# A quarter of the sums by source beside the filling of layer 0's slots, and layer 3's target factors spread over partitions by transfers

## The chip, the cores and the metric

The kernel runs on one core of one Trainium2 chip. The metric is the device time of one execution in microseconds, as the median of several runs; less is better. Of one execution there is also a profile, which the hardware profiler took; its times are microseconds from the start of the span. Engines are called PE (TensorE matmul), PEld (TensorE weight load), DVE (VectorE), ACT (ScalarE), POOL (GpSimd) and SP (SyncE, which here only issues transfers).

## The reference, cut to what matters

A graph network of four layers on 3125 nodes of 256 features and 100000 edges. Each layer adds a graph part and a mixing part, and then a feed-forward part, to x. Two pieces concern the change.

Layer 0's feed-forward part sends every node to its two best of 16 experts:

```python
topk_vals, topk_idx = jax.lax.top_k(gate_logits, K)          # K = 2, E = 16
topk_w = jax.nn.softmax(topk_vals, axis=-1)
h = jax.nn.relu(jnp.einsum('bsh,ehf->bsef', x, w1) + b1)
expert_out = jnp.einsum('bsef,efh->bseh', h, w2) + b2
moe = jnp.sum(topk_w[..., None] * sel, axis=2)               # sel: the two chosen experts' outputs
```

Layer 3's graph part is attention over edges with 4 heads of 64:

```python
e = jax.nn.leaky_relu(a_src[src] + a_dst[dst], 0.2)
alpha = softmax of e over the edges of each dst
out = jax.ops.segment_sum(alpha[:, :, None] * xp[src], dst, num_segments=n)
```

Layer 2's graph part needs, per source node, the sum of |edge_weight| over its edges. These are the "sums by source"; they depend on the inputs alone, so the kernel may compute them at any time before layer 2.

## The kernel before, in words

Nodes are kept as 25 blocks of 125 on partitions. `x` and `xn` are `[125, 25, 256]` tiles that live throughout; `xt` is the transposed copy. Columns are also cut into seven pieces: six of 500 nodes and one of 125. The kernel is written in a tile framework: the program text gives every instruction's place, and when the program is built a planner orders each engine's instructions by an estimate of when they can run, in case of doubt by their place in the text. On the chip each engine then works through its own list in that order. PSUM tiles named `ps` come from one pool of four banks, through `self.bank()`.

**Filling of layer 0's slots** (`l0_ffn`). The gates are sorted into slots: one tile of 384 slots belongs to one expert, and there are 26 tiles. A chain of small DVE operations ends in `slot` (L1113). POOL then issues 50 indirect transfers (L1116), which scatter the 25 blocks of `xn`, twice each, to `b0x_d` in memory. Meanwhile `times_rows` forms gates times the second bias and adds it to `xn` in place: per piece it transposes the gates (L290), copies them to `gt` (L162 or L164), multiplies (L296) and adds (L297). L297 overwrites `xn`, so it follows the scatters of its block.

**The tile loop** follows. For tile i, SP loads the expert's weights and the tile's rows (L1139 to L1145; the order on SP is written out by hand here), PE transposes the rows (L1150), DVE copies them (`xbt`, L1152), PE multiplies by w1 (L260), ACT applies Relu (L1157), PE multiplies by w2 (L1162), DVE and ACT copy the result (`yb`, L162 and L164), and ACT's queue stores it.

**The sums by source** (`weights_by_source`) run beside the tile loop as a generator. It loads sources and weights (L513, L515), prepares keys and three bf16 parts of the weights on DVE (L520 to L532), and then works through 782 columns of edges in 196 groups of four columns: `lo`, `oh` and three `ow` on DVE (L536 to L542), four matmuls of 128x128 by 75 on PE (L544), all into one accumulating bank. Pool `w_wk` holds three `lo`, `oh` and `ow` each. After every tile the loop lets it go on to the share (i + 1) / 26. Its DVE instructions are kept behind `filled`, the last L297.

**Layer 3's dense stage** (`l3_gnn_mix`, `l3_dense`). Edge counts have been laid out as a dense matrix `ctt_d`. For two pieces of target nodes (1000 columns) at a time, two heads at a time, the loop over 25 source blocks loads counts `cs` (L155, L156, three buffers), forms `t` by Relu on ACT (L1951), `z` on DVE (L1954), and multiplies by `xr` on PE into four accumulators (L1957). `rows`, which lies in the memory of `xn`, holds the target factors exp(0.8 a_dst + bias) of all four heads for the present pair, the same on all 125 partitions. They are made ahead of every pair: PE multiplies `xt` by the attention column, broadcast over the weights' columns (L1930), and ACT applies Exp (L1932). At the end of two heads, accumulators are copied, transposed (L1972) and finished on DVE (L1912 to L1919). The last pair is one piece of 125, taken with all four heads. A second generator, the mixing part, runs beside it: `together` lets the two alternate by their progress, the mixer ahead by a factor of 1.15.

Of the kernel before, what the change touches and what calls it, by code (L numbers as in the profile page):

```python
# [12 lines left out]
F32 = mybir.dt.float32  # L13
# [4 lines left out]
AF = mybir.ActivationFunctionType  # L18
OP = mybir.AluOpType
# [4 lines left out]
N = 3125  # L24
D = 256
P = 125
NB = 25
HB = D // 128
# [9 lines left out]
PW = 500  # L38
# [52 lines left out]
def _tables():  # L91


    t = np.zeros((NT1 * 128, 4), np.float32)
    t[:, 0] = N
    n = 0
    for b, (r, ws) in enumerate(WINDOWS):
        for d, w, k in ws:
            for j in range(k):
                t[n] = b * P + d, w, r, 128 * j  # L100
                n += 1
    t = np.concatenate([t, np.zeros((128, 4), np.float32)])
    t[NT1 * 128:, 0] = N
    t[NT1 * 128:NT1 * 128 + NB, 0] = np.arange(NB) * P
    return np.ascontiguousarray(t.reshape(NT1 + 1, 128, 4).transpose(1, 2, 0))
PIECES = [(i, min(PW, N - i)) for i in range(0, N, PW)]


class Net:
    NE, TS = 16, 384  # L110
# [938 lines left out]
    def l0_ffn(self, fast=False):  # L1049

        nc, tc, a = self.nc, self.tc, self.a
        NE, TS, ST, NT, bx = self.NE, self.TS, self.TS // 128, self.NT, self.bx
        by = self.dram.tile([NT * TS, D], F32, name="b0y_d")
        with ExitStack() as s:
            sb = s.enter_context(self.pool("f0_sb"))
            wk = s.enter_context(self.pool("f0_wk", 2))
            b2 = sb.tile([NE, D], F32, name="b2")
# [3 lines left out]
            g, w, i8 = self.top2(sb, None, NE, P, NB, self.greatest)  # L1061
# [17 lines left out]
            for e in range(NE):  # L1079
                nc.vector.tensor_tensor_scan(run[:, :, e], self.ones[:, :NB], tot[:, :, e], 0.0,  # L1080
                                             op0=OP.mult, op1=OP.add)
# [4 lines left out]
                                    op0=OP.mult)  # L1086
# [21 lines left out]
            slot = sb.tile([P, 2, NB], I32, name="slot")  # L1108
            sf = sb.tile([P, 2, NB], F32, name="slotf")
            for j in range(2):  # L1110
                nc.vector.tensor_mul(hot[j], hot[j], run[:P])
                nc.vector.tensor_reduce(sf[:, j, :], hot[j], axis=AX.X, op=OP.add)
            nc.vector.tensor_scalar(slot, sf, float(NT * TS - 1), None, op0=OP.min)  # L1113
            for b in range(NB):
                for j in range(2):
                    st = nc.gpsimd.indirect_dma_start(  # L1116
# [3 lines left out]
                    tc.add_to_no_dep_group("slots", st.ins)  # L1120
            self.add_rows(beta)
            y = self.xn
            filled = self.times_rows(sb, g, b2, NE, y, self.xn)
            with ExitStack() as s2:
                sums = None
                if fast:
                    sums = self.weights_by_source(s2.enter_context(self.pool("w_sb")),
                                                  s2.enter_context(self.pool("w_wk", 3)), self.bank())
                wk2 = s2.enter_context(self.pool("f0_t", 3))
                pl = s2.enter_context(self.pool("f0_ps", 4, space=PSUM))  # L1130
                s2.enter_context(tc.manual_schedule(engines={mybir.EngineType.SP}))

                def bank():
                    return pl.tile([128, 512], F32, name="pl")

                for i in range(NT):
                    e = nc.sync.value_load(own[0:1, i:i + 1], min_val=0, max_val=NE - 1)
                    w1 = wk2.tile([128, HB, 512], F32, name="w1")
                    nc.sync.dma_start(w1, a["L0_ffn_w1"][ds(e, 1)].rearrange("o (c p) f -> p (o c) f", p=128))  # L1139
                    b1 = wk2.tile([128, 4], F32, name="b1")  # L1140
                    nc.sync.dma_start(b1, a["L0_ffn_b1"][:, ds(e, 1), :].rearrange("p o f -> p (o f)"))
                    w2 = wk2.tile([128, 4, D], F32, name="w2")
                    nc.sync.dma_start(w2, a["L0_ffn_w2"][ds(e, 1)].rearrange("o (c p) f -> p (o c) f", p=128))
                    xb = wk2.tile([128, ST, D], F32, name="xb")
                    nc.sync.dma_start(xb, bx[i * TS:(i + 1) * TS].rearrange("(t p) d -> p t d", p=128))  # L1145
                    xt = wk2.tile([128, HB, TS], F32, name="xbt", bufs=2)
                    for h in range(HB):
                        ps = bank()
                        for t in range(ST):
                            nc.tensor.transpose(ps[:, t * 128:(t + 1) * 128], xb[:, t, h * 128:(h + 1) * 128],  # L1150
                                                self.ident)
                        nc.vector.tensor_copy(xt[:, h, :], ps[:, :TS])  # L1152
                    hid = wk2.tile([128, 4, TS], F32, name="hid", bufs=2)
                    for f in range(4):
                        ps = bank()
                        self.mm_feat(ps[:, :TS], w1[:, :, f * 128:(f + 1) * 128], xt, 0, TS)
                        nc.scalar.activation(hid[:, f, :], ps[:, :TS], AF.Relu, bias=b1[:, f:f + 1])  # L1157
                    yb = wk2.tile([128, ST, D], F32, name="yb", bufs=2)
                    for t in range(ST):
                        ps = bank()  # L1160
                        for f in range(4):
                            nc.tensor.matmul(ps[:, :D], hid[:, f, t * 128:(t + 1) * 128], w2[:, f, :],  # L1162
                                             start=(f == 0), stop=(f == 3))
                        self.evac(yb[:, t, :], ps[:, :D])
                    nc.scalar.dma_start(by[i * TS:(i + 1) * TS].rearrange("(t p) d -> p t d", p=128), yb)
                    if sums is not None:

                        with tc.issue_after(filled.ins):
                            for part in sums:
                                if i + 1 < NT and part > (i + 1) / NT:  # L1170
                                    break

            def gather(i, w_):
                for b in range(i // P, (i + w_) // P):
# [659 lines left out]
    def l3_gnn_mix(self, before, arrivals):  # L1834
# [5 lines left out]
        nc, a = self.nc, self.a  # L1840
        with ExitStack() as s:
            ms = s.enter_context(self.pool("m3_sb"))
            with self.pool("m3_w") as sb:
                w = self.load_w(sb, "L3_gnn_W")
# [36 lines left out]
            nc.vector.tensor_reduce(self.viol[:P, 6:7], over, axis=AX.X, op=OP.add)  # L1881
            nc.vector.tensor_tensor(bias, a8, bias, op=OP.min)

            us = sb.tile([P, 3, NB, 4], F32, name="us")
            nc.vector.tensor_sub(us[:, 2], al[:, :, :4], top[:, :, :4].to_broadcast([P, NB, 4]))
            nc.scalar.activation(us[:, 0], us[:, 2], AF.Exp)
            nc.scalar.activation(us[:, 1], us[:, 2], AF.Exp, scale=0.2)
            nc.vector.tensor_scalar(us[:, 2], us[:, 1], -1.0, None, op0=OP.mult)
            mix.send(mw)
            self.together([self.l3_dense(sb, wk, pa, wx, xr, us, bias), mix], (1.0, 1.15))  # L1890

    def together(self, parts, pace=(1.0, 1.0)):

# [5 lines left out]
            except StopIteration:  # L1899
                del at[p]  # L1900

    def l3_dense(self, sb, wk, pa, wx, xr, us, bias):

        nc = self.nc
        few = sb.tile([P, NB, 4], F32, name="few")
# [4 lines left out]
        def finish(b, h0, nh, acc):  # L1910
# [8 lines left out]
            nc.vector.scalar_tensor_tensor(v, t[:, :nh].rearrange("p h d -> p (h d)"), 0.0, v,  # L1919
                                           op0=OP.max, op1=OP.add)  # L1920

        done, there = 0, []
        for p0 in range(0, len(PIECES), 2):
            pcs = PIECES[p0:p0 + 2]
            n = sum(w for _, w in pcs)
            for h in range(4):
                for k, (i, w) in enumerate(pcs):
                    ps = self.bank()
                    for c in range(HB):
                        nc.tensor.matmul(ps[:P, :w], wx[:, c, 260 + h:261 + h].to_broadcast([128, P]),  # L1930
                                         self.xt[:, c, i:i + w], start=(c == 0), stop=(c == HB - 1))
                    nc.scalar.activation(rows[:, h, k * PW:k * PW + w], ps[:P, :w], AF.Exp, bias=bias[:, h:h + 1],  # L1932
                                         scale=0.8)
            hg = 4 if n < PW else 2
            for h0 in range(0, 4, hg):
                acc = {}
# [3 lines left out]
                for b in range(NB):  # L1940
# [20 lines left out]
                    if b == 5:  # L1961
                        for i in there:
                            self.arrive(i)
                        there = []
                if hg == 2:
                    for h in range(2):
                        for k, (i, w) in enumerate(pcs):
                            self.evac(at[:, h, k * PW:k * PW + w], acc[h, k][:, :w])
                    for j in range(n // P):
                        ps = self.bank()  # L1970
                        for h in range(2):
                            nc.tensor.transpose(ps[:P, h * 65:(h + 1) * 65], at[:, h, j * P:(j + 1) * P],  # L1972
                                                self.ident[:65, :65])
                        finish(p0 * 4 + j, h0, 2, ps[:P, :130].rearrange("p (h c) -> p h c", h=2))
                        yield done / (NB * N * 4)
                else:
                    for h in range(4):
                        self.evac(at[:, h // 2, h % 2 * P:(h % 2 + 1) * P], acc[h, 0][:, :P])
                    ps = self.bank()
                    for h in range(4):  # L1980
                        nc.tensor.transpose(ps[:P, h * 65:(h + 1) * 65], at[:, h // 2, h % 2 * P:(h % 2 + 1) * P],
                                            self.ident[:65, :65])
                    finish(p0 * 4, 0, 4, ps[:P, :260].rearrange("p (h c) -> p h c", h=4))
# [426 lines left out]
```

## Time and profile before

| | us |
|---|---|
| median of 3 runs | 4722.29 (4718.48 to 4723.53) |
| profiled execution | 4857.34 |
| its span | 4855.5 |
| PE busy in the span | 3791.1 (78%) |
| DVE busy | 2518.8 (52%) |
| ACT busy | 1321.2 (27%) |
| POOL busy | 1016.0 (21%) |
| L544, sums by source, on PE | 76.3 between 888 and 1290 |
| L1116, 50 scatters on POOL | 59.6 between 807 and 888 |
| L1930, target factors on PE | 47.3 |
| L1932, target factors on ACT | 17.3 |
| granted TensorE clock, mean | 0.859 |

A group of instructions in the profile is given by its line, engine and operation, what it writes and reads, shapes and count; then busy time and mean duration; then the idle time of the engine just before it and what ended that. Records of TensorE count a float32 product twice. A line can be that of a helper: L155, L162, L164, L260 and L297 serve many stages, so they are read by stretch of time.

### The profile page before, as it was taken

Reading aid. Unit: us, or ns where it says so; the run is one execution under the profiler, and the core shown is the slowest. Engines: PE = TensorE matmul, PEld = TensorE weight load, DVE = VectorE, ACT = ScalarE, POOL = GpSimd, SP = SyncE. Lnnn points to the kernel's source line nnn. Section 1 sums busy time; section 2 is a strip of 40 time slices with the busy share of each in tenths; the row PEclk is TensorE's granted clock in tenths of the full one; section 3 lists DMA queues with packets and bytes.
Section 4 is the critical chain, followed back from the end, with each engine's and each line's share of the span. In section 5 each row is a group of like instructions: output and inputs, shape, how many; then the busy total and the mean of one; then the engine's idle time right before and its main releaser. Section 6 shows DMA issues by size and latency. Waiting matters only on the chain. (4 is left out here: it accounts for less than half of the span.)

```text
span 4855.5 us, 50596 instructions
## 1 busy us (share of the span) xinstructions
PE 3791.1 (78%) x16806; PEld 2521.4 (52%) x16806; DVE 2518.8 (52%) x8603; ACT 1321.2 (27%) x2364; POOL 1016.0 (21%) x1041
## 2 busy tenths in 40 slices
PE   1886895799657899997454556676599999999798
PEld 0675894566534565555343445455364444444465
DVE  5886335445576319954222222343355667667544
ACT  1466100111123232333000000000154655556511
POOL 1000002200243000002666666666000000000011
PEclk8786996799878799998676777787799999999799
DMA  6245511433230000002333333333301112111132
GB/s 181 59 119 145 137 33 40 127 119 118 82 80 19 24 14 7 14 7 65 90 94 92 93 92 92 86 93 92 111 7 31 51 44 59 42 49 52 50 128 68
DMA packets 253461, 352.56 MB, mean 73 GB/s; under 512 B 61645, under 2 KB 198276, under 8 KB 253191
## 3 DMA queue, kind: packets, MB, share of 16 engines
q1 hardware_dynamic: 133326, 169.77, 12.1%
q0 software_dynamic: 62832, 126.93, 9.9%
q10 hardware_dynamic: 57033, 52.54, 4.0%
q8 instruction: 137, 2.24, 0.2%
q14 instruction: 133, 1.09, 0.1%
HBM read 262.48 MB, written 94.92 MB: 74 GB/s over the span
## 5 line engine op out<-in xcount | busy, mean ns | idle before, releaser
L1598 POOL DMA_INDIRECT hg<-hx_d,idx x782 | 743.0, 950 | 418.8 <-issue 209.7
L1614 PE MATMUL acc<-hg,to 128*125 128x256 f32 x2042 | 590.7, 445 | 280.7 <-issue 157.7
L1614 PEld LDWEIGHTS acc<-hg,to 128*125 128x125 f32 x2042 | 439.3, 222 | 411.1 <-issue 192.7
L1957 PE MATMUL acc<-z,xr 125*65 125x500 f32 (+1 forms) x1400 | 573.7, 552 | 10.5 <-DVE z L1954 8.6
L1609 DVE TENSOR_SCALAR to<-iota_w,rel_b,kw 128x125 f32<-128x125 f32 (+1 forms) x782 | 252.7, 378 | 454.9 <-remote 263.6
L1954 DVE SCALAR_TENSOR_TENSOR z<-t,us,cs 125x1000 f32<-125x1000 f32 (+1 forms) x400 | 410.2, 1029 | 136.2 <-PE acc L1957 103.3
L1951 ACT ACTIVATE t<-xn,us 125x1000 f32<-125x1000 f32 (+1 forms) x400 | 409.4, 1037 | 236.9 <-DVE z L1954 231.3
L1957 PEld LDWEIGHTS acc<-z,xr 125*65 125x65 f32 x1400 | 187.8, 143 | 313.2 <-issue 271.3
L260 PE MATMUL ps<-xt,w 128*128 128x500 f32 (+1 forms) x672 | 268.8, 547 | 1.8 <-DMA w<-in_L_ffn_W_dram 1.8
L1533 DVE SCALAR_TENSOR_TENSOR junk<-iota_w,rel_b,lock 128x125 f32<-128x125 f32 (+1 forms) x782 | 248.0, 384 | 0.0
L796 ACT ACTIVATE k<-k 125x128 f32<-125x128 f32 x50 | 15.8, 317 | 775.1 <-DVE k L795 542.8
L2240 POOL DMA_INDIRECT bx_d<-row,slot x25 | 31.2, 1247 | 923.3 <-ACT t L1951 809.4
L588 PE MATMUL ps<-y,cb 125*125 125x256 bf16 x1875 | 215.2, 280 | 0.0
L588 PEld LDWEIGHTS <-cb 125*125 125x125 bf16 x1875 | 214.0, 141 | 0.1
L189 ACT ACTIVATE rstd_t<-rstd_t 125x4 f32<-125x4 f32 (+2 forms) x86 | 17.2, 203 | 678.6 <-DVE rstd_t L188 622.1
L254 PE MATMUL ps<-wo,h 128*125 128x256 f32 x800 | 187.7, 386 | 3.6 <-ACT h L1436 2.6
L1442 DVE SCALAR_TENSOR_TENSOR x<-ps,lg,x 125x256 f32<-125x256 f32 x200 | 92.7, 480 | 173.5 <-PE ps L254 173.5
L260 PEld LDWEIGHTS ps<-xt,w 128*128 128x128 f32 x672 | 122.7, 193 | 114.5 <-issue 102.2
L260 PE MATMUL ps<-h,w 128*128 128x500 f32 (+1 forms) x448 | 179.5, 541 | 2.3 <-ACT h L1431 1.6
L254 PEld LDWEIGHTS ps<-wo,h 128*125 128x125 f32 x800 | 142.7, 187 | 66.0 <-ACT h L1436 43.7
L260 PE MATMUL pl<-xbt,w 128*128 128x384 f32 x416 | 169.9, 557 | 8.2 <-DVE xbt L1152 5.8
L469 PE MATMUL t<-ky,lo 128*128 128x75 bf16 (+4 forms) x1251 | 138.5, 253 | 38.6 <-ACT ct L472 24.5
(566 smaller groups left out, 6225.3 us busy)
## 6 DMA issues: line engine op xcount, KB each, us to landing
cs<-ctt_d SPq DMA_DIRECT2D x150, 218.8 KB
w<-in_L_ffn_w_dram SPq DMA_DIRECT2D x52, 512.0 KB
cnt_d<-cd SPq DMA_DIRECT2D x25, 683.6 KB
cb<-cnt_d SPq DMA_DIRECT2D x25, 683.6 KB
ctt_d<-ct ACTq DMA_DIRECT2D x6, 2734.4 KB
hg<-hx_d,idx POOLq DMA_INDIRECT x782
b0x_d<-zero SPq DMA_DIRECT2D x1, 9984.0 KB
xb<-b0x_d SPq DMA_DIRECT2D x26, 384.0 KB
```

The source lines that it names most:

```text
L254: self.nc.tensor.matmul(ps, xt[:, h, b * P:(b + 1) * P], w[:, h, :], start=(h == 0), stop=(h == k - 1))
L260: self.nc.tensor.matmul(ps, w[:, h, :], xt[:, h, i:i + n], start=(h == 0), stop=(h == k - 1))
L469: nc.tensor.matmul(t[:, w * 25 * r:(w + 1) * 25 * r], lo[:, :, n % 4], ky[:, :25 * r, n % 4], start=(j == 0), stop=(j == ws[w0 + w][2] - 1))
L588: nc.tensor.matmul(ps[:P, :D], cf[k][:, h * P:(h + 1) * P], y3[:, b0 + k, j, :], start=(k == 0 and j == 0), stop=(k == m - 1 and j == 2))
L1442: nc.vector.scalar_tensor_tensor(self.x[:, b, :], ps[:P, :D], g[:, b, e:e + 1], self.x[:, b, :], op0=OP.mult, op1=OP.add)
L1533: nc.vector.scalar_tensor_tensor(junk[:, :m * P], self.iota_w[:, :m * P], rel[:, c:c + 1], lock[:, b:b + m].rearrange("p b n -> p (b n)"), ...
L1598: nc.gpsimd.indirect_dma_start(out=hg[:, j, :], out_offset=None, in_=hx, in_offset=bass.IndirectOffsetOnAxis(ap=idx[:, c0 + j:c0 + j + 1], ...
L1609: nc.vector.tensor_scalar(to, self.iota_w[:, :nb * P], rel[:, c:c + 1], kw[:, j:j + 1], op0=OP.is_equal, op1=OP.mult)
L1614: nc.tensor.matmul(acc[k], to[:, (k - b) * P:(k - b + 1) * P], hg[:, j, :D], start=(c == first[k]), stop=(c == last[k]))
L1951: nc.scalar.activation(t[:, :n], rows[:, k4, :n], AF.Relu, bias=us[:, 2, b, k4:k4 + 1], scale=us[:, 0, b, k4:k4 + 1])
L1954: nc.vector.scalar_tensor_tensor(z[:, :n], t[:, :n], us[:, 1, b, k4:k4 + 1], c, op0=OP.add, op1=OP.mult)
L1957: nc.tensor.matmul(acc[h, k][:, :w], xr[:, b, k4, :], z[:, k * PW:k * PW + w], start=(b == 0), stop=(b == NB - 1))
```

## The change

Two parts.

The first part begins the sums before the tile loop. Their DVE instructions are now kept behind `placed`, the operation that writes `slot`, and not behind the last L297. Ahead of the tile loop, and outside the part in which SP's order is written out by hand, the generator is driven until its share exceeds `EARLY` = 0.25. In the loop, the shares run from there to 1.

The second part makes the target factors once: four exponentials of `[125, 25]` from `al`, a transpose, a copy and a store of `[100, 125]` to a tensor `r3_d` in memory. `target_rows` then loads 1000 columns of two heads from there, broadcast over 125 partitions, by SP: all four heads ahead of the first pair, and from then on two heads for the next pair, as soon as these heads of the present pair are through. The products L1930 and exponentials L1932 go.

```diff
+EARLY = 0.25
...
-            nc.vector.tensor_scalar(slot, sf, float(NT * TS - 1), None, op0=OP.min)
+            placed = nc.vector.tensor_scalar(slot, sf, float(NT * TS - 1), None, op0=OP.min)
...
-            filled = self.times_rows(sb, g, b2, NE, y, self.xn)
+            self.times_rows(sb, g, b2, NE, y, self.xn)
             with ExitStack() as s2:
                 sums = None
                 if fast:
                     sums = self.weights_by_source(s2.enter_context(self.pool("w_sb")),
                                                   s2.enter_context(self.pool("w_wk", 3)), self.bank())
+
+                    with tc.issue_after(placed.ins):
+                        for part in sums:
+                            if part > EARLY:
+                                break
...
-                    if sums is not None:
-
-                        with tc.issue_after(filled.ins):
-                            for part in sums:
-                                if i + 1 < NT and part > (i + 1) / NT:
-                                    break
+                    for part in sums or ():
+                        if i + 1 < NT and part > EARLY + (1 - EARLY) * (i + 1) / NT:
+                            break
...
+            r = sb.tile([P, 4, NB], F32, name="r3")
+            for h in range(4):
+                nc.scalar.activation(r[:, h], al[:, :, 4 + h], AF.Exp, bias=bias[:, h:h + 1], scale=0.8)
+            ps = self.bank()
+            nc.tensor.transpose(ps[:4 * NB, :P], r.rearrange("p h b -> p (h b)"), self.ident[:P, :P])
+            rt = sb.tile([4 * NB, P], F32, name="rt3")
+            nc.vector.tensor_copy(rt, ps[:4 * NB, :P])
+            r_d = self.dram.tile([4, N], F32, name="r3_d")
+            nc.sync.dma_start(r_d.rearrange("h (b p) -> (h b) p", p=P), rt)
+
             us = sb.tile([P, 3, NB, 4], F32, name="us")
...
-            self.together([self.l3_dense(sb, wk, pa, wx, xr, us, bias), mix], (1.0, 1.15))
+            self.together([self.l3_dense(sb, wk, pa, xr, us, r_d), mix], (1.0, 1.15))
...
+        def target_rows(i, h0):
+
+            n = min(2 * PW, N - i)
+            for h in (h0, h0 + 1):
+                if n > 0:
+                    self.move(nc.sync, rows[:P, h, :n], r_d[h, i:i + n].partition_broadcast(P))
+
         done, there = 0, []
+        for h0 in (0, 2):
+            target_rows(0, h0)
         for p0 in range(0, len(PIECES), 2):
             pcs = PIECES[p0:p0 + 2]
             n = sum(w for _, w in pcs)
-            for h in range(4):
-                for k, (i, w) in enumerate(pcs):
-                    ps = self.bank()
-                    for c in range(HB):
-                        nc.tensor.matmul(ps[:P, :w], wx[:, c, 260 + h:261 + h].to_broadcast([128, P]),
-                                         self.xt[:, c, i:i + w], start=(c == 0), stop=(c == HB - 1))
-                    nc.scalar.activation(rows[:, h, k * PW:k * PW + w], ps[:P, :w], AF.Exp, bias=bias[:, h:h + 1],
-                                         scale=0.8)
...
                 if hg == 2:
+                    target_rows(pcs[0][0] + 2 * PW, h0)
                     for h in range(2):
```

`move` issues two transfers for one tile: partitions 0 to 111, and the rest.

More of the change, by code (lines that the diff above doesn't have):

```diff
@@ L1900, in together, with l3_dense @@
                 del at[p]
-    def l3_dense(self, sb, wk, pa, wx, xr, us, bias):
+    def l3_dense(self, sb, wk, pa, xr, us, r_d):
         nc = self.nc
```

## The prediction

> **What bounds the kernel now.** I read the busy time by stretch first, then the groups of instructions, then the order of events on single engines. The change touches three stretches: the filling of the slots (807 to 888 us), the tile loop (888 to 1290) and layer 3's dense stage (3676 to 4590). Columns: busy us and (instructions) of PE, PEld, DVE, ACT, POOL, granted TensorE clock, DMA share, GB/s.
>
> ```profile
> 807.00:888.00 81.00, 28.95 (x63) 13.08 (x63) 14.58 (x31) 1.69 (x3) 59.64 (x50) 0.50 0.36 101
> 888.00:1290.00 402.00, 376.19 (x1924) 276.96 (x1925) 204.65 (x1058) 73.92 (x141) 0.00 (x0) 0.93 0.37 117
> 3676.00:3696.00 20.00, 18.58 (x44) 8.21 (x45) 5.29 (x12) 11.69 (x18) 0.00 (x0) 0.91 0.05 13
> 3696.00:4510.00 814.00, 800.71 (x2422) 354.18 (x2421) 547.31 (x1052) 471.01 (x534) 20.45 (x16) 1.00 0.19 49
> ```
>
> In the fill POOL issues 50 scatters back to back and everyone else idles. The tile loop has PE busy 376 of 402 us, the dense stage 801 of 814: both end when PE ends, and PE time taken out of them is time gained. The next lines are PE groups: busy us, mean ns, then idle before the group.
>
> ```profile
> L544 PE MATMUL ps<-ow,lo 128*128 128x75 bf16 x752 | 76.3, 249 | 17.4 <-DVE ow L542 15.6
> L1957 PE MATMUL acc<-z,xr 125*65 125x500 f32 (+1 forms) x1400 | 573.7, 552 | 10.5 <-DVE z L1954 8.6
> L1930 PE MATMUL ps<-xt,wx 128*125 128x500 f32 (+1 forms) x112 | 47.3, 587 | 0.9 <-DVE rd L1914 0.9
> ```
>
> L544 is the sums by source, L1930 the product that spreads the target factors. Who waits in the fill:
>
> ```profile
> DVE xn L297 <- DMA b0x_d<-xn,slot: 65.5, 25, 6.4
> PE ps L296 <- DVE xn L297: 18.4, 13, 2.2
> ```
>
> DVE's add L297 overwrites xn, so it waits for the scatters that read it, one block each 2.95 us; L296 waits in turn for the add to free one of the four shared banks.
>
> **What the Trainium skill says.** "SBUF — State Buffer", Who interferes with whom: a tensor_tensor has no mode that takes the port pair shared with GpSimd, copies, casts and tensor_scalars may. The sums' groups are tensor_tensor; only preparation (three casts, two tensor_scalars and a key cast, each 0.56 us) could hold up a scatter, 3.4 us at worst. No such overlap is in this trace. "TensorE: Matmul & The Clock Gate", Part 1: an idle PE runs at half clock; the fill's 0.50 agrees. "DMA: Bandwidth & Descriptors", Anatomy of one DMA: about 2.0 us plus bytes over 436 GB/s. The first xb load (384 KB) took from its issue at 884.61 to PE's start at 888.15, 3.5 us against an estimate of 2.9. The same page, Queues, rings and completion order: descriptors of one ring are consumed in order[...]; no run here shows it yet.
>
> **The sums, step by step.** A group is four matmuls; there are 196. EARLY takes 49 of them out of the loop: 196 of 784 matmuls. Each costs PE (76.3 + 17.4) / 752 = 0.125 us there, so the loop shortens by **24.4 us**, and by about 1 more as PE is warmer at its start. Bounds: 19 (busy time alone) to 26.
>
> What they cost outside depends on where they land. Memory they need was free long before (POOL's iota for them ran behind L593, ahead of the fill), so both input loads, now outside the hand-ordered SP list, can precede it instead of standing behind tile 0's xb. Preparation (8.5 us of DVE) then has idle time in the fill. The groups need more: an accumulator bank. It is requested after the 32 banks of times_rows, and the trace shows these four banks always taken: L290 and L296 follow strictly in program order, each upon an L297. So I take it that the accumulator gets a bank only when the last L296 has one, upon L297 of block 21, 9 us before the end. Until then DVE can make three groups, as lo has three buffers.
>
> The second limit is the order in DVE's queue, fixed at build by a planner's estimate:
>
> ```profile
> 827.89 0.42 DVE L297 TENSOR_TENSOR xn<-ps,xn 125x256 f32<-125x256 f32 x1 [2.49 <-DMA b0x_d<-xn,slot]
> 828.23 0.66 DVE L162 COPY gt<-ps 16x500 f32<-16x500 f32 x1
> ```
>
> L162's input was ready at 826.45, yet it stands behind an add that waited until 827.89: the planner took the scatter to be sooner than it was. So it leaves fewer gaps than there are, and about four groups fit behind block 21. Some 42 of 49 groups are left when the last add ends at 885.1. They come earlier in the program than tile 0, and this has a precedent: tile 1's copy L1152 stands at the end of tile 0's eight groups.
>
> ```profile
> 905.57 0.42 DVE L536 TENSOR_TENSOR lo<-i,key 128x512 bf16<-128x512 bf16 x1
> 905.91 0.45 DVE L542 TENSOR_TENSOR ow<-oh,part 128x100 bf16<-128x100 bf16 x3
> 906.27 0.21 DVE L538 TENSOR_TENSOR oh<-i,key 128x100 bf16<-128x100 bf16 x1
> 906.39 0.55 DVE L1152 COPY xbt<-pl 128x384 f32<-128x384 f32 x1
> ```
>
> From start to start a group takes DVE 0.34 (lo) + 0.12 (oh) + 0.36 (ow) = 0.82 us; PE needs 0.45 at full clock, 0.9 at half. So DVE sets the pace for 42 x 0.82 = 34.4 us before xbt of tile 0, with PE half idle. Today xbt starts 4 us after the last add, so the loop starts **30.4 us later**. Bounds: 0 (all 49 fit in the fill) to 49 x 0.82 + 3.4 = 43.6. Net for this part: 30.4 - 25.4 = **+5 us**.
>
> Queued behind these groups on DVE are L1152 and then all of tile 0. SP's loads of the first tiles wait for nothing there. The fill itself is POOL's and does not wait for L297.
>
> **The target factors, step by step.** Out go 112 L1930 records and 28 exponentials L1932. PE saves 47.3 us, in blocks of 13.6, 15.1, 15.3 and 3.4 us. ACT saves 17.3 us; it has slack (471 of 814), so I count nothing: L1957 covers it. In come four exponentials of 125x25, one transpose, one copy, one 50 KB store and broadcast loads: 2 x 4 x 4 = 32 issues.
>
> - First block: bias is ready at 3677.5. Four exponentials of about 0.28 (row L1886), transpose 0.27 (row L1865) and copy about 0.4: 3679.3. The store, an estimate from the DMA page, takes 2.1 and its issue 0.4; SP then issues eight loads at 0.3 and 0.43, and a head of 500 KB lands 3.2 after issue: about 3685.5 for the first, 3687 for the second. With Relu 1.22 and z 1.26 the first L1957 comes at about 3690 instead of 3695.3. PE idles from 3682 unless the mixer's keys and values (1.88 + 0.61 us a block) move in; I take one more block: **8 us** gained. Bounds: -5 (loads at a quarter of the rate) to 13.6.
> - Second and third: the rows are reloaded a group of 25 blocks ahead (over 80 us), so hidden. At the boundaries inside a pair, which have no L1930, PE stays full (30 of 30 us in 3800:3830), with mixer work and early z. L1930 also covered the eight finishing chains, 0.8 us each on DVE; that cover goes, z may be late by 2 us. **13 us** each. Bounds 8 and 15.
> - Last piece: heads 2 and 3 are reloaded only when Relu of the pair before is through; 125 columns, some 2.5 us, while the finishing takes 6. DVE is the limit here. **2 us** of 3.4; bounds 0 to 5.
>
> SP: at each group's end four issues wait for the last Relu, with the next counts (cs) queued behind them and DVE's z behind those. cs is loaded about two blocks ahead, 11 us where the mixer runs along; 1 MB takes 2.0 + 2.4 = 4.4 by the page. Hidden. Sum: 8 + 13 + 13 + 2 = **36 us**; bounds 11 to 48.
>
> **Total.** The profiled execution took 4857.3 us (span 4855.5 and 1.8 around it), 135 above the median of 4722.3. Saved: 36 - 5 = 31 of 4857, 30 at the median's scale: **4692 us**.
>
> **Rivals.**
> - *The groups do spread over the fill.* DVE idles 65.5 us there, and 8.5 + 49 x 0.82 = 49 would fit. Against it: the banks and the planner. Then -25 + 3 (scatters held up) - 36 = -58: 4664.
> - *The sums as forecast, the factors half effective*: PE starved at the boundaries, 15 us gained; +8 - 15 = -7: 4715.
> - *Slower:* the broadcast loads land ahead of cs at each group's end. If one source row read by 125 partitions comes at 35 GB/s, 1 MB takes 29 us, 18 beyond the 11 us of lead; four large reloads cost 72 less what z's three buffers hold (5 each), some 52. With +5 - 36 that is +21: 4743. It decides from a stall of 8 us a reload, a rate of 53 GB/s. For it: cs itself moves at 49 GB/s. Against: that is demand, at a DMA share of 0.19, so the engines have over 250 GB/s.
>
> **How the numbers follow.** Forecast 0.46, spread 0.24, half effective 0.15, slower 0.15. A difference of 0.2%, 9.4 us, is what a measurement of this kernel tells from none. The forecast's own range, with its bounds, is 4672 to 4714, nearly all faster; of the half effective case most is within 0.2%. Faster 0.72, same 0.13, slower 0.15. The range leaves out the slower case and a tail of the spread one: 4658 to 4722.
>
> **What would show it.** Right: no L1930; L1957 close behind the finishing transposes near 3950 and 4250; L544 starting only in the last 10 us of the fill, and L1152 of tile 0 some 30 us behind the last L297; a loop 24 us shorter. Wrong: L544 running from soon after the first scatters (the spread case), z waiting for cs at group ends (the slower one), or a scatter above 1.2 us.

## The result, and the profile after

| | before | after |
|---|---|---|
| median | 4722.91 us (4718.48 to 4725.31, 4 runs) | 4665.22 us (4663.24 to 4667.36, 4 runs) |
| profiled execution | 4857.34 us | 4666.18 us |
| its span, mean TensorE clock | 4855.5 us, 0.859 | 4664.4 us, 0.869 |

The ratio is 0.9879 (95% interval 0.9868 to 0.9891): 57.7 us less, where 31 were forecast. The two traces differ by 191 us, because layer 2's gathers took 1122 us from the first to the last in the profiled execution of before and 987 in that of after. That stage has two speeds, 135 us apart, which seem to go with the chip and not with the kernel (the four kernels of the first experiments, run on one chip, all showed the longer one, with 4857 us for the kernel before; the six others, on two other chips, all showed the shorter one). So the traces are compared by stage, and each kernel with the kernel before on its own chip.

Anchors for the stages: `slot` (L1113, now L1114), the first gather of `yg` after the tile loop, `bias` (L1882, now L1885) and the last product of the dense stage (L1957, now L1971), all by their starts.

| us | before | after | difference |
|---|---|---|---|
| `slot` to xbt of tile 0 | 82.1 | 118.0 | +35.9 |
| xbt of tile 0 to first `yg` | 410.5 | 352.2 | -58.3 |
| sum: `slot` to first `yg` | 492.6 | 470.2 | **-22.4** |
| `bias` to last dense product | 909.3 | 877.3 | **-32.0** |

The rest, about 3 us, lies in stretches that the change does not touch. The busy time by stretch of after, with the columns of the prediction's first fence:

```profile
808.00:889.00 81.00, 30.92 (x83) 14.66 (x84) 25.80 (x68) 1.70 (x3) 63.18 (x50) 0.50 0.34 93
889.00:926.00 37.00, 19.85 (x174) 14.68 (x174) 35.53 (x215) 0.00 (x0) 0.00 (x0) 0.50 0.28 90
926.00:1278.00 352.00, 343.12 (x1784) 258.39 (x1783) 163.52 (x835) 75.00 (x143) 0.00 (x0) 0.99 0.40 124
3518.00:3534.00 16.00, 13.52 (x33) 6.26 (x34) 3.48 (x8) 6.29 (x19) 0.00 (x0) 0.71 0.50 129
3534.00:4310.00 776.00, 763.94 (x2322) 337.88 (x2321) 540.21 (x1048) 454.96 (x506) 20.47 (x16) 0.99 0.21 57
```

Between fill and loop there is a new stretch of 37 us in which DVE works alone (35.53 busy) and PE is half idle at half clock. In the loop the granted clock is 0.99, where it was 0.93. The groups (busy, mean ns, idle before; L545 between 880 and 1280, L1971 over the span) and the waits from 807 on (us, times, longest):

```profile
L545 PE MATMUL ps<-ow,lo 128*128 128x75 bf16 x782 | 78.9, 249 | 30.1 <-DVE ow L543 27.4 <-DVE xn L298 0.9
L1971 PE MATMUL acc<-z,xr 125*65 125x500 f32 (+1 forms) x1400 | 577.4, 556 | 14.3 <-DVE z L1968 13.0
```

```profile
DVE xn L298 <- DMA b0x_d<-xn,slot: 54.0, 25, 5.3
PE ps L297 <- DVE xn L298: 19.0, 11, 2.4
PE ps L545 <- DVE xn L298: 0.9, 1, 0.9
```

The last line is the accumulator getting its bank from an add, as forecast; the first product of the sums starts at 880.9, the last scatter ended at 886.8. DVE's timeline then shows the groups ahead of tile 0, at the pace of 0.82 us, from the last add to xbt:

```profile
889.47 0.42 DVE L298 TENSOR_TENSOR xn<-ps,xn 125x256 f32<-125x256 f32 x1 [1.83 <-DMA b0x_d<-xn,slot]
889.82 0.44 DVE L543 TENSOR_TENSOR ow<-oh,part 128x100 bf16<-128x100 bf16 x3
890.17 0.42 DVE L537 TENSOR_TENSOR lo<-i,key 128x512 bf16<-128x512 bf16 x1
...
925.37 0.42 DVE L537 TENSOR_TENSOR lo<-i,key 128x512 bf16<-128x512 bf16 x1
925.70 0.45 DVE L543 TENSOR_TENSOR ow<-oh,part 128x100 bf16<-128x100 bf16 x3
926.07 0.21 DVE L539 TENSOR_TENSOR oh<-i,key 128x100 bf16<-128x100 bf16 x1
926.19 0.56 DVE L1158 COPY xbt<-pl 128x384 f32<-128x384 f32 x1
```

So the sums did not spread over the fill, and still the time is that of the rival in which they do (4664). It came from the loop: 58 us shorter, not 25.

In layer 3 the L1930 blocks are gone. PE's timeline at the third pair (before, 15.25 us of L1930 stood here):

```profile
4069.80 1.00 PE L1971 MATMUL acc<-z,xr 125*65 125x500 f32 x2
4070.64 0.56 PE L1987 MATMUL ps<-ident,xn 65*125 65x65 f32 x4
4071.52 2.14 PE L1321 MATMUL ps<-bd,q_e 128*125 128x132 f32 x12 [0.32 <-DVE rd L1927]
4074.44 3.57 PE L1971 MATMUL acc<-z,xr 125*65 125x500 f32 x8 [0.78 <-DVE z L1968]
```

After the finishing transposes L1987 come the mixer's products (L1321) and the next pair, with 1.1 us of idle time. Over the whole stage z waited for cs once:

```profile
DVE z L1968 <- DMA cs<-ctt_d: 2.2, 1, 2.2
```

### The profile page after: what moved, and what is told of

It reads as the page before. It is cut to its first block, busy times and chain, and to the rows that moved or that the text cites. A ratio compares the mean times of both kernels' runs of the same rounds, so it can differ in the third digit from the quotient of the medians.

```text
span 4664.4 us, 50401 instructions
## 1 busy us (share of the span) xinstructions
PE 3722.3 (80%) x16695; PEld 2505.9 (54%) x16695; DVE 2505.6 (54%) x8604; ACT 1302.8 (28%) x2336; POOL 1020.2 (22%) x1041
## 5 line engine op out<-in xcount | busy, mean ns | idle before, releaser
L1617 PEld LDWEIGHTS acc<-hg,to 128*125 128x125 f32 x2042 | 455.4, 227 | 309.3 <-DVE to L1612 216.3
L1971 PE MATMUL acc<-z,xr 125*65 125x500 f32 (+1 forms) x1400 | 577.4, 556 | 14.3 <-DVE z L1968 13.0
L1971 PEld LDWEIGHTS acc<-z,xr 125*65 125x65 f32 x1400 | 188.9, 145 | 314.8 <-issue 265.5
L1605 DVE TENSOR_TENSOR kw<-hg,awt 128x8 f32<-128x8 f32 x98 | 16.4, 168 | 581.2 <-DMA hg<-hx_d,idx 513.2
L261 PE MATMUL ps<-xt,w 128*128 128x500 f32 (+1 forms) x672 | 269.0, 547 | 1.8 <-DMA w<-in_L_ffn_W_dram 1.8
L243 PE MATMUL ps<-ident,xn 125*128 125x125 f32 x300 | 58.8, 347 | 159.8 <-DVE xn L209 159.7
L261 PEld LDWEIGHTS ps<-xt,w 128*128 128x128 f32 x672 | 122.7, 193 | 114.7 <-issue 102.4
L261 PE MATMUL ps<-h,w 128*128 128x500 f32 (+1 forms) x448 | 179.5, 541 | 2.3 <-ACT h L1434 1.6
```

What stands on the lines that cost most here:

```text
L243: self.nc.tensor.transpose(ps[:, j * P:(j + 1) * P], src[:, i // P + j, h * 128:(h + 1) * 128], self.ident[:P, :P])
L261: self.nc.tensor.matmul(ps, w[:, h, :], xt[:, h, i:i + n], start=(h == 0), stop=(h == k - 1))
L1617: nc.tensor.matmul(acc[k], to[:, (k - b) * P:(k - b + 1) * P], hg[:, j, :D], start=(c == first[k]), stop=(c == last[k]))
L1971: nc.tensor.matmul(acc[h, k][:, :w], xr[:, b, k4, :], z[:, k * PW:k * PW + w], start=(b == 0), stop=(b == NB - 1))
```

## The experiments

Time against the kernel before on the same chip; the third column is the stage from `slot` to the first `yg` in the run's own trace (before: 492.6).

| run | change of median, us | ratio (95% interval) | `slot` to `yg`, us |
|---|---|---|---|
| sums_alone | -26 | 0.9947 (0.9933 to 0.9960) | 472.4 |
| factors_alone | -33 | 0.9936 (0.9923 to 0.9950) | 491.5 |
| early_14 | -58 | 0.9876 (0.9861 to 0.9891) | 471.0 |
| kept_warm | -9 | 0.9983 (0.9976 to 0.9989) | 484.4 |
| kept_dense | -17 | 0.9963 (0.9949 to 0.9976) | 474.8 |
| own_bank_first | -54 | 0.9890 (0.9875 to 0.9905) | 474.6 |
| rows_twice | -50 | 0.9892 (0.9877 to 0.9907) | 472.2 |
| first_by_pe | -44 | 0.9909 (0.9894 to 0.9924) | 471.5 |
| paced_two | -82 | 0.9822 (0.9808 to 0.9835) | 439.7 |
| paced_one | -67 | 0.9857 (0.9842 to 0.9872) | 458.1 |

**Which part brought it.** `sums_alone` is the kernel before with the diff's first part, `factors_alone` with its second.

> Only the first part of the change, factors as before. Clock theory (my reading of the traces of before and after): the loop starts 36 us later, as the prediction's working had it (30), but is 58 us shorter and not 25, because with 5 to 6 groups a tile PE no longer idles and its clock stays at 1.00: 22 us faster than before, about 4700. Rival, the prediction's own sum: 5 us slower, about 4727, and then the factors must have brought 60.

> Only the second part, sums as before. Clock theory: the stretch from bias to the last product of the dense stage is 32 us shorter in the trace of after, so 30 to 34 us faster than before, about 4690. Rival (the sums brought nothing): 55 to 63 us faster, about 4663.

Measured -26 and -33, together -59: the parts add up, and the prediction's +5 for the sums is out. (In the single traces the two stages give -20 and -32.)

**Why the loop is shorter than its groups explain.** From the first L260 of one tile to that of the next, a tile that carries 5, 6, 7 or 8 groups takes 13.0, 13.65, 14.4 and 15.3 us, unless its L260 runs slowly, and then some 1.6 us more or, in a few tiles, over 2. Before, tiles had 7 or 8 groups in turn, and 13 of the 25 distances from tile to tile were above 15.4 us; after, none. In the traces the granted clock of this loop is always 1.00 or 0.50 and changes only in steps of a multiple of 3.41 us. With windows on that grid, one slow start of a tile of before looks so (the clock is the third number from the right):

```profile
1014.03:1017.44 3.41, 2.35 (x27) 2.03 (x25) 3.41 (x21) 0.00 (x0) 0.00 (x0) 1.00 0.62 177
1017.44:1020.85 3.41, 3.21 (x12) 1.92 (x12) 3.41 (x19) 0.00 (x0) 0.00 (x0) 0.50 0.60 212
1020.85:1024.26 3.41, 3.41 (x12) 1.95 (x11) 0.73 (x6) 1.65 (x3) 0.00 (x0) 1.00 0.00 0
```

Each of the 13 slow distances holds 2.8 to 6.0 us at 0.50, the 12 others at most 0.8. Together the loop of before has 52.6 us at half clock, that of after 3.0, all in its first tile.

The theory was a clock that falls after an 8-group gap. Two kernels tested it. `early_14` is the changed kernel with 7 groups in every tile:

```diff
-EARLY = 0.25
+EARLY = 14 / 196
```

> The changed kernel with EARLY = 14/196: 14 groups ahead of the loop, 7 in every tile, none with 8. Clock theory: seven groups a tile leave PE's gaps short enough for the full clock (a tile of 14.4 us), so the loop is 25 us longer than in the changed kernel (35 groups at 0.7) but starts 29 us earlier (35 x 0.82): 4 us faster than the changed kernel, about 4661, clock 1.00 in the loop. Rival, a gain in proportion to the groups moved (58 us / 49 = 1.19 each): 41 us longer, 29 earlier, 12 us slower than the changed kernel, about 4677, clock about 0.95.

It equals the changed kernel (0.9876 and 0.9879). Its loop, from the first L260 of tile 0 to that of tile 25, is 366.4 us against 337.0 (+29) and starts 29 us earlier; 3 distances of 25 are slow. The 12 us that a gain in proportion would cost are outside the interval. The forecast gain of 4 us is too small to be told from none; by the trace, the three slow distances took it. So 35 of the 49 early groups brought nothing: DVE takes 0.82 us for each ahead of the loop, and the loop gives back as much.

`kept_warm` adds work to the kernel before, in 13 tiles with 8 groups (all but the first), where PE waits: two matmuls behind the fifth group and six behind the sixth.

```diff
+            self.nth += 1
+            for j in range(self.fillers.get(self.nth, 0)):
+                nc.tensor.matmul(spare[:, :3 * NB], lo[:, :, j % 4],
+                                 ow[:, :, :, j % 4].rearrange("p k h -> p (k h)"), start=True, stop=True)
```

> The kernel before with more work: in the 13 tiles with 8 groups, 8 further matmuls of the same shape into a bank that nothing reads are put where PE waits for ow (2 after the fifth group, 6 after the sixth; 0.9 us a tile). Clock theory: PE doesn't idle there, the clock stays at 1.00, the mean of L260 in the loop falls from 0.556 to about 0.49 us and the loop gets some 20 us SHORTER in spite of 104 more matmuls: about 4702. Rival (L260 is slow for another reason, traffic of the loads or DVE's accesses, or because the profile puts waits into it): no gain, 4722, or up to 12 us slower, 4734.

It is faster, but by 9 us, not 20: 10 slow distances are left of 13. That led to a second form, with matmuls of 512 columns (one and three, the product of lo with lo) in the same places.

> The kernel before with fillers as in kept_warm, but dense ones: in the 13 tiles with 8 groups, 1 + 3 matmuls of 128x128 by 512 (0.21 us each at full clock) into a bank that nothing reads, where kept_warm had 2 + 6 of 75 columns. Theory of a clock that follows how densely PE works within a window of 3.4 us: 11 of 12 intervals behind an 8-group gap were slow before and 6 with kept_warm, because matmuls of 75 columns are as sparse as a wait; dense ones leave at most 3 slow ones, so the loop is 13 to 18 us shorter than before, ratio about 0.9965. Rival (only the time without any matmul counts): as kept_warm, 5 to 9 us, ratio 0.998 to 0.999.

It gave 17 us, with 3 slow distances. The group of L260 between 905 and 1280 for before, for after (L261, 940 to 1260) and for kept_dense with its fillers (L548):

```profile
L260 PE MATMUL pl<-xbt,w 128*128 128x384 f32 x384 | 156.4, 556 | 7.7 <-DVE xbt L1152 5.3 <-issue 2.3
```

```profile
L261 PE MATMUL pl<-xbt,w 128*128 128x384 f32 x384 | 129.9, 492 | 1.1
```

```profile
L260 PE MATMUL pl<-xbt,w 128*128 128x384 f32 x400 | 144.2, 505 | 8.2 <-DVE xbt L1155 5.8 <-issue 2.3
L548 PE MATMUL ps<-lo 128*128 128x512 bf16 x48 | 17.1, 396 | 0.0
```

The mean of the same product falls from 556 to 505 ns by work that nothing reads, and the clock of `kept_dense` stays up through most of its loop:

```profile
912.38:1236.64 324.26, 309.26 (x1706) 231.52 (x1706) 167.33 (x883) 62.77 (x120) 0.00 (x0) 1.00 0.40 123
```

In PE's timeline, before and kept_dense at the same place:

```profile
1017.38 0.44 PE L544 MATMUL ps<-ow,lo 128*128 128x75 bf16 x4 [0.71 <-DVE ow L542]
1018.02 1.62 PE L260 MATMUL pl<-xbt,w 128*128 128x384 f32 x2 [0.20 <-issue]
```

```profile
1013.39 0.45 PE L544 MATMUL ps<-ow,lo 128*128 128x75 bf16 x4 [0.38 <-DVE ow L542]
1014.03 0.88 PE L260 MATMUL pl<-xbt,w 128*128 128x384 f32 x2 [0.19 <-issue]
```

Two L260 take 1.62 us after the gap of 0.71 and 0.88 after the filled one. Waits alone don't decide, or the sparse fillers would have done as much as the dense ones. The Trainium skill ("TensorE: Matmul & The Clock Gate", Part 1) describes a free-running window of about 3.4 us, after which an idle PE falls to half clock. The 3.41 us and the 0.50 of these traces agree. But here PE was never idle for a window: the stretch of groups and transposes between L1162 and L260 is 4.6 us in a tile with 8 groups (3.2 or less with 5 or 6), and PE idled for 1.2 of it, in three gaps. In the loop of before (900 to 1275), PE was busy for 63 to 74% of each of the 12 windows that come just ahead of a fall, and for 76% or more of every other window at full clock. In `kept_warm` eight of nine falls came behind windows of 77 to 82%, so the busy share alone is not the rule. That what counts is how much of the array is at work fits the two fillers, but is not shown, and where the threshold lies stays open.

**Why the early groups don't run beside the fill.** `own_bank_first` removes the reason that the prediction gave, the bank, and puts the early groups ahead of times_rows:

```diff
+                acc = s2.enter_context(self.pool("w_ps", 1, space=PSUM)).tile([128, 512], F32, name="wacc")
...
-                pl = s2.enter_context(self.pool("f0_ps", 4, space=PSUM))
...
+                bank = self.bank
```

> The changed kernel, with an accumulator bank of the sums' own (the tile loop takes the four shared banks instead of four of its own) and the 49 early groups ahead of times_rows in the text. Bank theory: the 36 us by which the loop starts later are the groups that find no bank during the fill; with one, all 49 run beside the scatters, the loop starts 3 to 10 us later than before (preparation 3.5, scatters held by tensor_tensors up to 0.13 us each), so 26 to 32 us faster than the changed kernel, ratio to before about 0.982. Rival (DVE's accesses hold the scatters, 0.3 us each, or the adds L298 pile up behind the groups and delay tile 0): 10 to 15 us faster than the changed kernel, ratio about 0.985 to 0.986; the scatters' mean would be 1.5 us.

No gain: 0.9890. The groups now start at 817.6, but POOL's timeline holds one scatter of 40 us, and DVE's shows what ran beside it:

```profile
818.60 39.94 POOL L1117 DMA_INDIRECT b0x_d<-xn,slot  x1 [0.30 <-issue]
858.84 1.18 POOL L1117 DMA_INDIRECT b0x_d<-xn,slot  x1 [0.30 <-issue]
```

```profile
817.62 0.41 DVE L537 TENSOR_TENSOR lo<-i,key 128x512 bf16<-128x512 bf16 x1
...
857.62 0.55 DVE L543 TENSOR_TENSOR ow<-oh,part 128x100 bf16<-128x100 bf16 x3
857.98 0.52 DVE L298 TENSOR_TENSOR xn<-ps,xn 125x256 f32<-125x256 f32 x1
862.64 0.42 DVE L298 TENSOR_TENSOR xn<-ps,xn 125x256 f32<-125x256 f32 x1 [4.14 <-DMA b0x_d<-xn,slot]
```

The scatter ends at 858.54, when DVE, which had not rested since 817.6, has ended its last add (858.50) and waits at last. Neither theory had that: the rival foresaw 1.5 us for each. The median scatter is still 1.19 us. Meanwhile the DMA engines had next to nothing to move (the last two numbers: their busy share, GB/s), so it was POOL's issue of the transfer that was held, not the transfer:

```profile
822.00:858.00 36.00, 19.80 (x177) 14.19 (x177) 36.00 (x223) 0.00 (x0) 36.00 (x1) 0.50 0.01 1
```

`paced_two` keeps the bank and breaks the run, with two groups behind each add but the first; `paced_one` has one group there. From their edits:

```diff
                 last = nc.vector.tensor_add(out[:, b, :], ps[:P, :D], add[:, b, :])
+                if beside is not None:
+                    beside(b, last)
...
+                def beside(b, add):
+                    with tc.issue_after(add.ins):
+                        for _ in range(PER_ADD if b >= FROM else 0):
+                            next(sums)
```

> As own_bank_first (a bank of the accumulator's own), but the early groups are tied to the adds L298: two behind each of the last 24, 48 in all, so that DVE rests between them. In own_bank_first one scatter took 39.9 us, as long as DVE ran tensor_tensors without a rest. Theory that only an unbroken run locks POOL out: each gap holds 1.6 us of DVE work and a scatter is held by 0.1 to 0.3 us at most, so the fill grows by 4 to 10 us, the loop starts 10 us later than in the kernel before instead of 36 to 44, and stays as short as in the changed kernel: 20 to 30 us faster than the changed kernel, ratio to before 0.982 to 0.984. Rival (every tensor_tensor holds POOL for its own length): the fill grows by 35 to 40 us and nothing is gained over the changed kernel, ratio 0.988 to 0.990.

> As paced_two, with one group behind each of the last 24 adds; 172 groups remain for the loop, 6 or 7 a tile, which leaves the clock at 1.00 in nearly all tiles. If only an unbroken run locks POOL out: the loop is 17 us longer than in paced_two (24 groups at 0.7) and the fill 2 to 5 us shorter: 12 to 15 us slower than paced_two, ratio 0.985 to 0.987. If every tensor_tensor holds POOL for its own length: the fill is 18 us shorter than in paced_two, which balances the loop: equal to paced_two within 3 us.

`paced_two` gives 0.9822, 82 us under the kernel before and 27 under the changed one by the ratios: the fastest version here. xbt of tile 0 comes 87.1 us after `slot`, where it was 82.1 before and 118.0 after, and the loop is the same (337.3 us between first and last L260, 337.0 after). POOL and DVE side by side:

```profile
829.00 1.22 POOL L1121 DMA_INDIRECT b0x_d<-xn,slot  x1 [0.31 <-issue]
830.52 1.21 POOL L1121 DMA_INDIRECT b0x_d<-xn,slot  x1 [0.30 <-issue]
```

```profile
828.61 0.42 DVE L299 TENSOR_TENSOR xn<-ps,xn 125x256 f32<-125x256 f32 x1 [1.08 <-DMA b0x_d<-xn,slot]
828.95 0.44 DVE L547 TENSOR_TENSOR ow<-oh,part 128x100 bf16<-128x100 bf16 x3
829.31 0.42 DVE L541 TENSOR_TENSOR lo<-i,key 128x512 bf16<-128x512 bf16 x1
829.64 0.20 DVE L543 TENSOR_TENSOR oh<-i,key 128x100 bf16<-128x100 bf16 x1
829.76 0.41 DVE L541 TENSOR_TENSOR lo<-i,key 128x512 bf16<-128x512 bf16 x1
830.10 0.44 DVE L547 TENSOR_TENSOR ow<-oh,part 128x100 bf16<-128x100 bf16 x3
830.46 0.20 DVE L543 TENSOR_TENSOR oh<-i,key 128x100 bf16<-128x100 bf16 x1
831.46 0.42 DVE L299 TENSOR_TENSOR xn<-ps,xn 125x256 f32<-125x256 f32 x1 [0.79 <-DMA b0x_d<-xn,slot]
```

DVE works for some 2 us of every 2.9 and rests 0.8 to 1.1; beside the groups the scatters keep 1.2 us. `paced_one` is 15 us behind `paced_two`, as the theory of an unbroken run has it (12 to 15), not equal to it. The times fit that theory, but the lines above don't fit its plain form, in which a scatter waits until DVE rests: the one of 829.00 ended at 830.22, while DVE worked on to 830.66. 16 scatters of this trace lie wholly inside such runs, of 2 to 3 us, and took 1.19 to 1.38 us. So it is shown that the long run came with a held scatter and that short ones did not; what in the long run held it stays open.

**The factors, step by step.** `first_by_pe` makes the first pair's factors as before (with the products of L1930 and the exponentials of L1932), `rows_twice` issues every load of `target_rows` twice:

```diff
+            for h in range(4 if p0 == 0 else 0):
+                for k, (i, w) in enumerate(pcs):
...
+                    for _ in range(2):
                         self.move(nc.sync, rows[:P, h, :n], r_d[h, i:i + n].partition_broadcast(P))
```

> The changed kernel with the first pair's factors made by PE and ACT as before (L1930's 32 matmuls, 13.6 us), the later pairs by transfers. If the first block gained 8 us, as the prediction's step says (because the mixer's work fills PE while the rows come): 6 to 10 us slower than the changed kernel. If it gained only the 2.4 us by which the first product of the dense stage comes earlier after bias: 1 to 4 us slower.

> The changed kernel with every load of target rows issued twice (32 more issues on SP, twice the bytes). If the loads are hidden, as the prediction holds: 0 to 4 us slower than the changed kernel, and these at the start of the dense stage (8 more issues by 0.37 = 3 us). If they stand ahead of the counts cs (the prediction's slower rival): 10 to 30 us slower, with DVE z waiting for cs at the group ends.

By the stage from `bias` to the last product (after: 877.3), `first_by_pe` takes 885.1, 7.8 more, and `rows_twice` 879.9, 2.6 more. In four of the five other kernels with these factors the stage takes 876.7 to 877.5, in `own_bank_first` 872.5. By the ratios the two stand 14 and 6 us behind the changed kernel, each with an interval of some 7 us to either side; in their traces both reached `bias` 6.5 to 6.8 us later, in stretches that are alike. In `first_by_pe` PE does this between `bias` (3524.7) and the first product of the stage:

```profile
3531.18 0.68 PE L1293 MATMUL ps<-va,k_e 125*128 125x129 f32 x4 [1.30 <-DVE k_e L1270]
3531.70 13.58 PE L1950 MATMUL ps<-xt,wx 128*125 128x500 f32 x32
3545.12 3.52 PE L1977 MATMUL acc<-z,xr 125*65 125x500 f32 x8
```

In the changed kernel the first product comes after 15.6 us, only 2.4 earlier than before, but by then the mixer has 14 more records of its 128x512 products done (0.43 us from start to start at full clock, 6.0 us): the gain is taken later, in the stage itself.

## Why the prediction was right or wrong

- **The direction of the whole was right; that of the sums was wrong.** 57.7 us were gained and 31 forecast. The factors gave 32.0 (forecast 36). The sums gained 22.4, where a loss of 5 was forecast. Had this error gone the other way, the whole would have been near nothing: that the total came out on the right side is owed to the factors, and for the sums to luck.
- **Loop, 24.4 us: mis-sized.** From the first L260 of tile 0 to that of tile 25 the loop is 57.9 us shorter (394.9 to 337.0). The step "each costs PE 0.125 us" failed twice. A group costs the tile 0.65 to 0.9 us, not 4 x 0.125 = 0.5, since DVE (0.82) paces a part of it. With all tiles at full clock the 25 distances of before (12 of 14.4, 13 of 15.3) would be 371.7, and those of after (whose first tile lost at most half of its 3.0 us at half clock) about 336. So the groups account for some 36 and the clock for some 22. The time at half clock gives an estimate beside it: 49.6 us less of it are worth at most half, 24.8. The trace of before had it: 0.93 in the fence, a mean of 556 ns for L260, the shortest ones in the loop at 486. The prediction gave "about 1" for a warmer PE.
- **Start of the loop, 30.4 us later: right.** Measured 35.9: the last add is 3.5 later after `slot`, and from its end to xbt are 36.3 us instead of 4. Three groups' lo stood ahead of block 21's add, as forecast.
- **The hold-up of the scatters, at most 3.4 us: the sum right, the parts not.** POOL's busy time rose by 3.5, and all but some 0.3 of it beside the preparation, as forecast. But the operations on the prediction's list brought only some 0.8. The largest part was not on it: beside the two operations that open the preparation (a memset of 1.04 us, then a scalar_tensor_tensor of 0.91) the first scatter took 3.04 us. And the prediction took a tensor_tensor for harmless. It quoted one half of the page: the Trainium skill ("SBUF — State Buffer", Who interferes with whom) also says that two inputs from SBUF contend with GpSimd's reads. In the changed kernel that did no harm, since its long run of groups came behind the last scatter; beside the run of `own_bank_first` one took 39.94. Whether it was this contention is not shown, as the same operations in short runs held none.
- **The spread rival** gave the measured number by another mechanism. Its price, "3 (scatters held up)", would have been met only with paced groups, which come to -82 and not -58, as the loop gives more.
- **First block of the factors, 8 us: the sum right** (7.8 by `first_by_pe`), its parts not: the first product came 2.4 us earlier and not 5.3, and the mixer moved in for some 6 us and not for one block of 2.5. **Boundaries, 13 + 13 + 2: nearly**, 24.2 = 32.0 - 7.8; they were not measured apart.
- **Rows ahead of cs, hidden: right.** Twice the loads cost 2.6 us, and z waited for cs 2.2 us in all, as in the changed kernel. The slower rival's 35 GB/s, an assumption, is refuted: from 3523 to 3531, with only these loads under way, the trace has 233 GB/s at a DMA share of 0.92. The Trainium skill ("DMA: Bandwidth & Descriptors", Anatomy of one DMA) gives the formula that the prediction used, 2.0 us plus bytes over 436 GB/s, for transfers that GpSimd issues. These are SP's: from the issue of the store to that of the first load there were 1.6 us, where the formula estimates 2.1.
- **A slip in a rival.** The half effective case says "the sums as forecast" and counts +8 for them, where the forecast is +5; it should be 4712 and not 4715.

## What to carry to other kernels

Price work that is taken out of a loop by the loop's own period (tiles with more and fewer pieces stand side by side in the trace), and look whether the granted clock there is below 1: the gain can be more than PE's own time for the work (here 57.9 us in the loop, where 24.4 were counted). Before DVE work is put beside an engine that issues indirect transfers, ask how long DVE would run without a rest; here small portions, tied to something that DVE waits for anyway, held nothing up, and one long run did. A time that agrees with a story says nothing on its mechanism until the parts are run apart.

## What the runs showed of the hardware

- An indirect transfer of POOL (1.19 us) took 39.94 us while DVE ran bf16 tensor_tensors with both inputs in SBUF back to back, and ended when that run ended; the DMA engines stood still meanwhile (share 0.01). With rests of about 1 us in every 2.9 the same instructions held none, and transfers that lay wholly inside a run of 2 to 3 us took 1.19 to 1.38 us. What the long one waited for was not separated.
- The granted clock of PE in the tile loop was 1.00 or 0.50 and changed only on a grid of 3.41 us. It fell for one such stretch, at times two, after 4.6 us in which PE was 75% busy, with transposes and matmuls of 75 columns. 52 dense matmuls more made the kernel faster by 17 us; 104 sparse ones by 9.
- A row of target factors, read from memory by 125 partitions, came at 233 GB/s over eight loads.
- In the trace of `own_bank_first` the recorded duration of lo drifts from 0.41 to 0.52 us during the 40 us, while the distance from start to start stays 0.82.
